# Sorted tokens of a mixture of experts: results scattered back by the row's own number instead of gathered

## The chip, the cores and the metric

The kernel runs on one core of a Trainium2 chip. TensorE is called PE, VectorE DVE, ScalarE ACT, GpSimd POOL and SyncE SP. Times are device microseconds of one launch; the measure is the median of repeated runs. A profile of one execution gives the times of single instructions.

## The reference, cut to what matters

The input is 32 images of 128 channels and 56 x 56 positions, in float32. A binary convolution and an attention-like layer come first. Then each of an image's 3136 positions is a token of 128 values, and a router sends it to two of eight experts:

```python
router_probs = jax.nn.softmax(x @ router_w + router_b, axis=-1)
top_p, top_i = jax.lax.top_k(router_probs, K)          # K = 2 of E = 8
top_p = top_p / jnp.sum(top_p, axis=-1, keepdims=True)
expert_out = jnp.einsum('bnd,edc->bnec', x, expert_w) + expert_b
gathered = jnp.take_along_axis(expert_out, top_i[..., None], axis=2)
return jnp.einsum('bnk,bnkc->bnc', top_p, gathered)
```

The result is added to the token and returned with channels ahead of positions.

## The kernel before, in words

**Two ways through the experts.** An image's tokens are cut into 25 chunks of up to 128 tokens, four chunks to a block. The first chunks of an image go the dense way: all eight experts are computed for every token (`gated` on DVE at L1141, `experts` on PE at L1159), each token's input multiplied by its gates, which SP loads from DRAM spread over all partitions (`spread`, L1132, into the ring `bc` of four buffers). The last 17 or 13 chunks of images 0 to 27 go the sorted way; images 28 to 31 are all dense.

**The sorted way.** Images form four groups of 8, 8, 8 and 4. There are 28 pairs of experts, and each group has a table `rows` in DRAM with a region for each pair. Per image, `pair_of` finds each token's pair and writes `hot`, which has a one at the token's pair (L1256). `places` (L1278 to L1293) finds each token's place in its pair's region by matmuls: `before`, a triangle of ones, counts the tokens ahead of it in its own chunk, and `ones_h` adds the chunks ahead of that one, four chunks at a time through `hot_sum`, which `hot_blocks` makes on POOL for images 0 to 7 (L1268) and on DVE for the others (L1272). `count_on` and `count_rest` keep the running count of the group for the next image. `row_numbers` (L1313 to L1318) turns places into rows. `row_scalars` writes two gates and an offset twice beside the token's 128 values (L1346), and `scatter` (L1365) writes a chunk's rows of 132 values to `rows` with an indirect DMA on POOL.

When a group is full, `list_1` to `list_4` make the list of its tiles, 128 rows of one pair each, and `pad` writes zero rows behind the end of each region. Four tiles make a quad: 40, 40, 32 and 20 quads in the groups, 132 in all. `tile_load` on SP reads a quad, `tile_turn` and `tile_turned` transpose it, `tile_experts` (L1687) multiplies by the two experts, `tile_read` on ACT applies the gates into `v` and `w` (rings of three and two buffers), `tile_sum` and `tile_out` on DVE (L1717, L1722) add them and the token, and `tile_store` on SP (L1730) writes the quad to a table `res` in the order of the tiles.

To bring the results back, `result_rows` on DVE (L1423 to L1439) computes for each token the row of `res` that holds its result; `gather` (L1444) reads each chunk's rows with an indirect DMA on POOL into one of 14 buffers `back`; `back_turn` on PE (L1459), `back_out` on ACT and `back_store` on SP transpose and store a block.

**The order of the work.** All engines run instructions in a written order. A planner makes it ahead of the launch: every step has an engine, a price in microseconds, a due time, the steps it follows and the buffers it takes and frees, and `in_order` lists the steps as if each engine worked through them at these prices, the most urgent of those that could start at about the same time first. `TILE_PACE` and `GATHER_PACE` spread a group's tiles and its gathers over time. On POOL, an indirect DMA also waits for the fourth indirect DMA ahead of it (`in_turn`, `IN_FLIGHT`).

Of the kernel before, what the change touches and what calls it, by code (L numbers as in the profile page):

```python
# [54 lines left out]
C = 128  # L55
# [23 lines left out]
ON_POOL = 8  # L79
# [4 lines left out]
GATE_LANDS, SPREAD_LANDS, STORE_LANDS, TILE_LANDS, GATHER_LANDS = 5.0, 6.5, 5.0, 6.0, 12.0  # L84
TILE_PACE = (0.7, 0.6, 0.4, 0.3)
GATHER_PACE = (1.0, 0.8, 0.5, 0.4)
N_Q = C + 2 * N_EXP
Q_GROUP = 3

# [9 lines left out]
    ps=5, acc=1, ff=2, y=3, qs=3, tt=4, bc=4, gt=2, gated=2,  # L99
    t_in=3, turned=2, v=3, w=2, back=12, sent=4, o=2,  # L100
# [85 lines left out]
def conv_attn_moe_kernel(  # L186
# [45 lines left out]
    n_list = 2  # L232
    assert max(group_rows) // C + N_PAIR <= n_list * C
# [20 lines left out]
    m_one = const.tile([C, 2], F32, name="m_one")  # L254
    nc.vector.memset(m_one, -1.0)


    member = bpool.tile([C, C // GROUP], F32, tag="back", bufs=14, name="member")
# [18 lines left out]
    bk_bc = bpool.tile([C, C], F32, tag="back", bufs=14, name="bk_bc")  # L277
# [147 lines left out]
    no_row = const.tile([C, most], F32, name="no_row")  # L425
    zeros = const.tile([C, ROW], F32, name="zeros")

    count = const.tile([C, N_PAIR], F32, name="count")
    count_h = const.tile([C, 2, N_PAIR], BF16, name="count_h")


    hot_all = const.tile([C, most + 1, N_PAIR], BF16, name="hot")
    hot_sum = const.tile([C, most // PER, N_PAIR], BF16, name="hot_sum")

    def prepare_sorted():
        nc.gpsimd.memset(hot_all, 0.0)
        nc.vector.memset(count_h, 0.0)
# [21 lines left out]
        nc.vector.tensor_scalar(tile_row, tile_no, float(C), None, ALU.mult)  # L459
        nc.vector.memset(no_row, 0.0)  # L460
# [83 lines left out]
    def plan_image(i: int):  # L544
# [578 lines left out]
        def spread(b, k):  # L1123
            n = cols_of(b)[1] - cols_of(b)[0]
            if k == 0:
                gt = bpool.tile([n_g, WIDE], BF16, tag="gt", bufs=2, name=f"gt_{i}_{b}")
                rows = d["gb"][b, :, :, :n].rearrange("j e t -> (j e) t")
                for r in range(0, n_g, n_g // 3):
                    nc.sync.dma_start(gt[r : r + n_g // 3, :n], rows)
                d["gt", b] = gt  # L1130
            bc = bpool.tile([C, 2, WIDE], F32, tag="bc", bufs=4, name=f"bc_{i}_{b}_{k}")
            nc.sync.dma_start(  # L1132
                bc[:, :, :n],
                d["gp"][b, 2 * k : 2 * k + 2, :n].unsqueeze(0).to_broadcast([C, 2, n]),
            )
            d["bc", b, k] = bc
# [93 lines left out]
        group = group_of[i]  # L1230
        first_of_group = i == 0 or group_of[i - 1] != group
        sort = slice(n_dense, n_ck)
        hot = hot_all[:, most - n_sort :, :]
        n_full = n_sort // PER

        def pair_of():
            high, low, pair = (
                spool.tile([C, n_sort], F32, tag=t, bufs=n, name=f"{t}_{i}")
                for t, n in (("high", 1), ("low", 1), ("pair", 13))
# [17 lines left out]
                hot[:, :n_sort, :],  # L1257
# [5 lines left out]
        def hot_blocks():  # L1263
            t = hot[:, : n_full * PER, :].rearrange("p (b k) q -> p b k q", k=PER)
            total = hot_sum[:, :n_full, :]
            with nc.allow_low_precision(reason="numbers up to four"):
                if i < ON_POOL:
                    nc.gpsimd.tensor_tensor(total, t[:, :, 0], t[:, :, 1], ALU.add)  # L1268
                    for k in range(2, PER):
                        nc.gpsimd.tensor_tensor(total, total, t[:, :, k], ALU.add)  # L1270
                else:
                    nc.vector.tensor_reduce(total, t.rearrange("p b k q -> p b q k"), AX.X, ALU.add)  # L1272

        def places():


            p = ps.tile([C, n_sort + 1, N_PAIR], F32, tag="ps", name=f"places_{i}")
            nc.tensor.matmul(p, lhsT=before, rhs=hot, start=True, stop=False)  # L1278
            if not first_of_group:
                for j in range(2):  # L1280
                    nc.tensor.matmul(
                        p,
                        lhsT=ones_h[:1],
                        rhs=count_h[:1, j].unsqueeze(1).to_broadcast([1, n_sort + 1, N_PAIR]),
                        start=False,
                        stop=False,
                    )

            counted = [(hot[:, c, :], c + 1, min(n_sort + 1, c // PER * PER + PER)) for c in range(n_sort)]
            counted += [(hot_sum[:, b, :], (b + 1) * PER, n_sort + 1) for b in range(n_full)]  # L1290
            counted = [(t, lo, hi) for t, lo, hi in counted if lo < hi]
            for t, lo, hi in counted:
                nc.tensor.matmul(  # L1293
                    p[:, lo:hi, :],
                    lhsT=ones_h,
                    rhs=t.unsqueeze(1).to_broadcast([C, hi - lo, N_PAIR]),
                    start=False,
                    stop=lo == counted[-1][1] and hi == counted[-1][2],
# [3 lines left out]
        def count_on():  # L1302
            nc.scalar.copy(count, d["places"][:, n_sort, :])
            nc.scalar.copy(count_h[:, 0], d["places"][:, n_sort, :])

        def count_rest():
            nc.vector.tensor_sub(count_h[:, 1], count, count_h[:, 0])

        def row_numbers():
            shape = [C, n_sort, N_PAIR]  # L1310
            own = spool.tile(shape, F32, tag="own", bufs=1, name=f"own_{i}")
            place = spool.tile([C, n_sort], F32, tag="place", bufs=13, name=f"place_{i}")
            nc.vector.tensor_tensor(own, hot[:, :n_sort, :], d.pop("places")[:, :n_sort, :], ALU.mult)  # L1313
# [7 lines left out]
            d["place"] = place  # L1321

        def row_scalars():
# [3 lines left out]
            def tmp(tag):  # L1327
# [17 lines left out]
            pair_shape = [C, n_sort, 2]  # L1345
            nc.vector.tensor_tensor(  # L1346
                row[:, :, C + 2 : ROW],
                a.unsqueeze(2).to_broadcast(pair_shape),
                m_one.unsqueeze(1).to_broadcast(pair_shape),
                ALU.mult,  # L1350
# [11 lines left out]
        def scatter(c):  # L1362
# [15 lines left out]
            after=[("route_3", i), ("row_numbers", i - 1), ("places", i - 1), ("result_rows", i - 13)],  # L1378
        )
        at(  # L1380
            s + 132.5, ("hot_blocks", i), "POOL" if i < ON_POOL else "DVE",
            2.0 if i < ON_POOL else 0.048 * n_sort, hot_blocks, after=[("pair_of", i)],
        )
        at(
            s + 133, ("places", i), "PE", 0.3 + 0.08 * n_sort, places,
            after=[("hot_blocks", i), ("count_rest", i - 1), ("list_1", group - 1)], take=["ps"],
        )
        at(s + 135, ("count_rest", i), "DVE", 0.10, count_rest, after=[("count_on", i)])
        at(s + 134, ("count_on", i), "ACT", 0.22, count_on, after=[("places", i)])
        at(  # L1390
            s + 137, ("row_numbers", i), "DVE", [0.033 * n_sort, 0.034 * n_sort, 0.09], row_numbers,
            after=[("places", i), ("count_on", i), ("scatter", i - 2, n_ck - 1)],
            free=[("ps", ("places", i))],
# [5 lines left out]
        for k, c in enumerate(range(n_dense, n_ck)):  # L1399
# [6 lines left out]
                s + 140 + 2 * k, ("scatter", i, c), "POOL", 1.5, scatter, c,  # L1406
# [11 lines left out]
        def result_rows():  # L1418

            shape = [C, n_sort, N_PAIR]  # L1420
            own = spool.tile(shape, F32, tag="own2", bufs=1, name=f"own2_{i}")
# [456 lines left out]
```

## Time and profile before

| | |
|---|---|
| three runs | 2249.86, 2259.04, 2283.94 us; median 2259.04 |
| the profiled execution | 2270.18 us, of which the span from first to last instruction is 2268.4 |
| busy in the span | PE 93%, DVE 87%, ACT 68%, POOL 46% |
| granted clock of PE, mean | 0.975 |
| indirect DMAs on POOL | 428 scatters, mean 1225 ns; 428 gathers, mean 1134 ns |
| group 0's tiles, first to last | about 505 to 870 us |
| gathers, first to last | 874 to 2241 us |

In a group's row the columns are line, engine, operation, result and operands, shapes and count; then busy microseconds and the mean of one in ns; then the engine's idle time just before, with what ended it. A row of waits names the engine and line that waited, what it waited for, and the sum, the number and the longest of the waits. The lines are those of the kernel before.

### The profile page before, as it was taken

To read this page: it belongs to the slowest core of one execution; us is meant where nothing else is said; L and a number is where in the kernel's file an instruction comes from. 1 tells how busy PE (TensorE), PEld (TensorE's weight loads), DVE (VectorE), ACT (ScalarE), POOL (GpSimd) and SP (SyncE) were. 2 spreads that over 40 slices of the span, in tenths; PEclk is the share of its full clock that TensorE was granted. 3 is DMA by queue.
4 is the path that set the end of the run, shared out by engine and by line. 5 is a ranking of instruction groups with operands and counts; after the bars stand their busy time and mean duration, and the time that the engine had idled before them with its cause. 6 is when DMAs were issued, how large, how long until landed. Compare 5 with 4: busy or idle time off the path is not lost.

```text
span 2268.4 us, 45320 instructions
## 1 busy us (share of the span) xinstructions
PE 2103.4 (93%) x12074; PEld 1449.1 (64%) x12074; DVE 1970.1 (87%) x6074; ACT 1531.2 (68%) x4917; POOL 1041.1 (46%) x1013
## 2 busy tenths in 40 slices
PE   5899999899999999789999999988999999999888
PEld 2666656557777776457676776655676666676544
DVE  4899999999989999688888889988898798789865
ACT  5667776668888887468777867655877776574311
POOL 3044443333433325466443644676654446233563
PEclk9989999999999999899999999999999999999999
DMA  4155544465665565377667766667767777878788
GB/s 166 30 175 177 167 153 141 138 184 184 203 186 165 176 181 168 110 219 252 194 202 220 226 198 202 215 214 240 225 195 232 217 203 247 249 214 270 222 278 273
DMA packets 324364, 448.58 MB, mean 198 GB/s; under 512 B 61832, under 2 KB 222128, under 8 KB 324112
## 3 DMA queue, kind: packets, MB, share of 16 engines
q1 hardware_dynamic: 294384, 382.80, 54.7%
q0 software_dynamic: 28144, 56.14, 8.2%
q10 hardware_dynamic: 1584, 6.75, 0.8%
q8 instruction: 102, 1.67, 0.3%
q14 instruction: 150, 1.23, 0.2%
HBM read 319.51 MB, written 126.00 MB: 196 GB/s over the span
## 4 chain that ended last, share of the span: by engine, by line
PE 42%; DVE 5%; DMA 3%; issue 2%; ACT 2%; another core or an unknown queue 1%; SPq 0%; POOL 0%; DVEq 0%; ACTq 0%; POOLq 0%
PE ff L1159 14%; PE to L1687 7%; PE cv L642 6%; PE q L863 3%; PE gram L744 3%; PE turn L1669 2%; PE back_ps L1459 2%; PE xt L667 2%; DVE gated L1141 1%; DMA back<-res,res_no 1%; PE l L1114 1%; DMA out_dram<-o 1%; PE ff L1153 1%; DMA bc<-gp 0%
## 5 line engine op out<-in xcount | busy, mean ns | idle before, releaser
L1365 POOL DMA_INDIRECT rows<-tok,row_no x428 | 524.3, 1225 | 570.5 <-ACT tok L1358 235.8
L1159 PE MATMUL ff<-gated,ew_d 128*128 128x512 f32 (+1 forms) x1536 | 711.5, 592 | 23.8 <-DVE gated L1141 19.8
L1444 POOL DMA_INDIRECT back<-res,res_no x428 | 485.4, 1134 | 464.1 <-PE back_ps L1459 264.1
L1141 DVE TENSOR_TENSOR gated<-tt,bc 128x1024 f32<-128x1024 f32 x384 | 450.7, 1180 | 92.2 <-PE ff L1159 29.9
L642 PE MATMUL cv<-xs,w_bin 128*128 128x440 bf16 (+3 forms) x2016 | 429.8, 362 | 18.5 <-ACT xs L599 10.0
L1159 PEld LDWEIGHTS ff<-gated,ew_d 128*128 128x128 f32 x1536 | 274.5, 193 | 258.6 <-issue 202.2
L1705 ACT ACTIVATE v<-to,t_in 128x128 f32<-128x128 f32 x528 | 255.3, 484 | 138.1 <-PE to L1687 74.6
L642 PEld LDWEIGHTS <-w_bin 128*128 128x128 bf16 x2016 | 200.1, 100 | 187.8 <-issue 38.3
L1687 PEld LDWEIGHTS to<-ew_s,turned 128*128 128x128 f32 x2112 | 260.8, 194 | 57.8 <-issue 32.4
L877 ACT ACTIVATE qs<-q,r 128x136 f32<-128x136 f32 (+1 forms) x800 | 247.6, 406 | 70.3 <-PE q L863 35.1
L1687 PE MATMUL to<-ew_s,turned 128*128 x2112 | 273.3, 279 | 18.2 <-ACT turned L1675 8.1
L735 ACT ACTIVATE y<-tok,r 128x128 f32<-128x128 f32 (+1 forms) x800 | 257.0, 428 | 24.3 <-PE gram L744 10.4
L863 PE MATMUL q<-move,x 128*128 128x144 f32 (+1 forms) x1600 | 239.9, 295 | 12.7 <-issue 3.7
L863 PEld LDWEIGHTS q<-move,x 128*128 128x128 f32 (+1 forms) x1600 | 213.6, 193 | 42.4 <-issue 21.1
L744 PEld LDWEIGHTS gram<-y 128*128 128x128 f32 (+1 forms) x1600 | 203.3, 192 | 53.9 <-issue 40.4
L744 PE MATMUL gram<-y 128*128 128x129 f32 (+1 forms) x1600 | 217.8, 281 | 12.9 <-issue 8.1
L682 DVE BATCH_NORM_STATS2 st<-tok 128x6 f32<-128x128 f32 (+1 forms) x800 | 185.4, 279 | 31.9 <-ACT tok L673 26.9
L1712 ACT ACTIVATE w<-to,t_in 128x128 f32<-128x128 f32 x528 | 208.6, 395 | 0.0
L893 DVE BATCH_NORM_STATS2 st<-tok 128x6 f32<-128x128 f32 (+1 forms) x800 | 198.1, 284 | 6.3
L673 ACT COPY tok<-xt 128x512 f32<-128x512 f32 (+1 forms) x224 | 121.2, 561 | 99.9 <-PE xt L667 71.6
L653 DVE SCALAR_TENSOR_TENSOR x<-cv,alpha_col,x 128x448 f32<-128x448 f32 x224 | 151.3, 676 | 40.1 <-PE cv L642 7.2
L890 DVE TENSOR_TENSOR tok<-tok,qs 128x408 f32<-128x408 f32 (+1 forms) x288 | 156.1, 542 | 29.4 <-ACT tok L882 24.1
(229 smaller groups left out, 2896.0 us busy)
## 6 DMA issues: line engine op xcount, KB each, us to landing
bc<-gp SPq DMA_DIRECT2D x368, 512.0 KB
x<-in_x_dram SPq DMA_DIRECT2D x116, 392.0 KB
t_in<-rows SPq DMA_DIRECT2D x528, 66.0 KB
res<-v SPq DMA_DIRECT2D x132, 256.0 KB
out_dram<-o SPq DMA_DIRECT2D x100, 256.0 KB
out_dram<-tt SPq DMA_DIRECT2D x92, 256.0 KB
rows<-zeros SPq DMA_DIRECT2D x116, 66.0 KB
rows<-tok,row_no POOLq DMA_INDIRECT x428
```

The costliest lines, as they stand in the source:

```text
L642: nc.tensor.matmul(cv[:, r0:r1, c0:c1], lhsT=w_bin[:, t, :], rhs=xs[:, b * ROWS + dy + r0 : b * ROWS + dy + r1, dx + c0 : dx + c1], start= ...
L735: nc.scalar.mul(y[:n, j, :C], d["tok"][:n, c, :C], d["r1"][:n, c : c + 1])
L744: nc.tensor.matmul(d["gram"], lhsT=y[:n, j, :C], rhs=y[:n, j, :], start=(c == 0), stop=(c == n_ck - 1),)
L863: nc.tensor.matmul(p[:n, k, :], lhsT=d["x"][:, c * C : c * C + n], rhs=move, start=True, stop=True,)
L877: nc.scalar.mul(qs[:n, k, :], p[:n, k, : C + N_EXP], d["r1"][:n, c : c + 1])
L1141: nc.vector.tensor_tensor(g[:, :, :n], d["tt", b][:, :n].unsqueeze(1).to_broadcast([C, 2, n]), d.pop(("bc", b, k))[:, :, :n], ALU.mult,)
L1159: nc.tensor.matmul(d["ff", b][:, :n], lhsT=ew_d[:, e * C : (e + 1) * C], rhs=g[:, j, :n], start=False, stop=(e == N_EXP - 1),)
L1365: dma = nc.gpsimd.indirect_dma_start(out=groups[group]["rows"], out_offset=bass.IndirectOffsetOnAxis(ap=d["row_no"][:n, c - n_dense : c - ...
L1444: dma = nc.gpsimd.indirect_dma_start(out=d["back", c][:n, :], out_offset=None, in_=groups[group]["res"][: quads_of(group) * WIDE, :], in_o ...
L1687: nc.tensor.matmul(p[:, k, j, :], lhsT=t[:, n * C : (n + 1) * C], rhs=ew_s[:, bass.ds(d["cols", q][j][n], C)], start=True, stop=True,)
L1705: nc.scalar.activation(d["v", q][:, n, :], p[:, k, 0, :], AF.Identity, bias=row[:, C + 2 : C + 3], scale=row[:, C : C + 1],)
L1712: nc.scalar.mul(d["w", q][:, n, :], p[:, k, 1, :], row[:, C + 1 : C + 2])
```

## The change

Four things are changed. The row of a token carries, in its last place, the number of a row in `res` that belongs to the token: a first part of `res` has a row for each place of a tile (for the rows that only fill a tile), and behind it stand the images of the group, chunk by chunk. `tile_out` takes the larger of that number and the number of the row's own place, and `send` writes each tile to `res` with an indirect DMA on POOL, four to a quad, in place of the one `tile_store` on SP. The results of a block then lie in order, so that `fetch`, a plain load on SP, takes the place of `result_rows` and the gathers; `back` has three buffers of a block each in place of 14 of a chunk.

Places are counted by partition first: `run_on` adds up `hot` chunk by chunk within each partition on POOL, `places` then needs two matmuls and, after a group's first image, a third for the running count, and `ranks` on POOL adds the two parts together, one per pair, for `row_numbers` to pick from.

The ring `bc` has five buffers. The planner's prices and paces change with it (`SEND` 1.3 for an indirect DMA that was priced at 1.5, `TILE_PACE` longer for all groups).

```diff
-ON_POOL = 8
+RUN, RANK = 0.20, 0.10
-TILE_PACE = (0.7, 0.6, 0.4, 0.3)
+TILE_PACE = (0.9, 0.8, 0.6, 0.4)
+BACK = 3
+SEND = 1.3
-    ps=5, acc=1, ff=2, y=3, qs=3, tt=4, bc=4, gt=2, gated=2,
-    t_in=3, turned=2, v=3, w=2, back=12, sent=4, o=2,
+    ps=5, acc=1, ff=2, y=3, qs=3, tt=4, bc=5, gt=2, gated=2,
+    t_in=3, turned=2, v=3, w=2, back=BACK, sent=4, o=2,
...
-        def hot_blocks():
...
+        def run_on():
+
+            with nc.allow_low_precision(reason="numbers up to the chunks of an image"):
+                for c in range(n_sort):
+                    nc.gpsimd.tensor_tensor(run[:, c + 1], run[:, c], hot[:, c], ALU.add)
 
         def places():
-            p = ps.tile([C, n_sort + 1, N_PAIR], F32, tag="ps", name=f"places_{i}")
-            nc.tensor.matmul(p, lhsT=before, rhs=hot, start=True, stop=False)
+            p = ps.tile([C, 2, N_PAIR], F32, tag="ps", name=f"places_{i}")
             if not first_of_group:
...
+                nc.tensor.matmul(
+                    p,
+                    lhsT=both,
+                    rhs=count_h.unsqueeze(1).to_broadcast([n_part, 2, N_PAIR]),
+                    start=True,
+                    stop=False,
+                )
+            for j, lhs in enumerate((before, ones_h)):
+                nc.tensor.matmul(
+                    p[:, j], lhsT=lhs, rhs=run[:, n_sort], start=first_of_group, stop=first_of_group or j == 1
+                )
...
+        def ranks():
+            shape = [C, n_sort, N_PAIR]
+            d["own"] = spool.tile(shape, F32, tag="own", bufs=1, name=f"own_{i}")
+            nc.gpsimd.tensor_tensor(
+                d["own"], run[:, :n_sort], counts[:, 0].unsqueeze(1).to_broadcast(shape), ALU.add
+            )
...
-            nc.vector.tensor_tensor(own, hot[:, :n_sort, :], d.pop("places")[:, :n_sort, :], ALU.mult)
+            nc.vector.tensor_tensor(own, hot, own, ALU.mult)
...
+            nc.vector.tensor_scalar(row[:, :, C + 2], a, -1.0, None, ALU.mult)
+            nc.vector.tensor_scalar(
+                row[:, :, C + 3], row_of[:, :n_sort], float(first_row * C), None, ALU.add
+            )
...
-        def result_rows():
...
-        def gather(c):
...
+        def fetch(b):
+            n, cs = rows_of(blocks[b][0]), blocks[b]
+            d["back", b] = bpool.tile([C, PER, C], F32, tag="back", bufs=BACK, name=f"back_{i}_{b}")
+            first = (first_row + cs[0] - n_dense) * C
+            rows = groups[group]["res"][first : first + len(cs) * C, :]
+            nc.sync.dma_start(
+                d["back", b][:n, : len(cs), :], rows.rearrange("(k p) c -> p k c", p=C)[:n]
+            )
...
+            at(
+                due + each * k / n_sort, ("fetch", i, b), "SP", 0.43, fetch, b,
+                after=[("send", group, q, k) for q in range(quads_of(group)) for k in range(PER)]
+                + [("fetch", i, b - 1) if k else ("fetch", i - 1, n_blk - 1)],
+                take=["back"], delay=FETCH_LANDS,
+            )
...
+        nc.vector.tensor_tensor(
+            d["no", q], d["in", q][:, :, C + 3], row_of[:, q * PER : (q + 1) * PER], ALU.max
+        )
...
-    def tile_store(g, q):
+    def send(g, q, k):
...
+        nc.gpsimd.nop()
+        dma = nc.gpsimd.indirect_dma_start(
+            out=d["res"],
+            out_offset=bass.IndirectOffsetOnAxis(ap=d["no", q][:, k : k + 1], axis=0),
+            in_=d["v", q][:, k, :],
+            in_offset=None,
+        )
+        alone(f"res{g}", dma, in_turn(dma))
...
+            for k in range(PER):
+                at(
+                    due + 12 + k, ("send", g, q, k), "POOL", SEND, send, g, q, k,
+                    after=[("tile_out", g, q), ("send", g, q, k - 1) if k else ("send", g, q - 1, PER - 1)]
+                    + ([("fetch", last_of[g - 2], n_blk - 1)] if q == k == 0 and g > 1 else []),
+                    free=[("v", ("tile_read", g, q, 0))] if k == PER - 1 else [], delay=3.0,
+                )
```

## The prediction

> **What bounds the kernel now.** I first read the engine shares of the page, then the busy time in stretches.
>
> ```profile
> PE 2103.4 (93%) x12074; PEld 1449.1 (64%) x12074; DVE 1970.1 (87%) x6074; ACT 1531.2 (68%) x4917; POOL 1041.1 (46%) x1013
> ...
> 140.00:490.00 350.00, 330.72 (x1860) 214.59 (x1858) 343.12 (x1210) 237.63 (x795) 157.02 (x144) 0.99 0.47 153
> 560.00:840.00 280.00, 275.56 (x1812) 205.75 (x1811) 262.58 (x822) 239.97 (x785) 92.98 (x73) 1.00 0.59 175
> 910.00:950.00 40.00, 29.94 (x111) 16.14 (x109) 23.32 (x78) 20.23 (x61) 21.79 (x22) 0.76 0.39 116
> 1400.00:1540.00 140.00, 129.51 (x695) 83.57 (x694) 123.08 (x406) 80.18 (x260) 99.98 (x83) 0.96 0.64 204
> 2100.00:2240.00 140.00, 119.68 (x445) 67.13 (x445) 99.13 (x197) 29.86 (x87) 83.96 (x73) 0.91 0.82 266
> ```
>
> The columns of a stretch are PE, PEld, DVE, ACT and POOL busy, then granted clock, DMA share and GB/s. Before the first tiles (140 to 490 us) DVE is busy 98% and sets the pace; beside the tiles of group 0 (560 to 840) PE is, at 98%; in the last stretch neither is full. So microseconds taken from PE count after about 500 us, and hardly before. POOL is nowhere the bound, yet its queue is in order, and each of its 856 indirect DMAs costs about 0.3 us between instructions on top of its busy time.
>
> Then the waits that end PE's idle time after the start (us in total, times, longest):
>
> ```profile
> PE ff L1159 <- DVE gated L1141: 19.8, 20, 2.6
> PE xt L667 <- DVE x L653: 9.6, 10, 1.7
> ...
> PE to L1687 <- ACT turned L1675: 8.1, 5, 3.4
> ```
>
> Nothing in this list names POOL: before the change nobody on PE's path waits for GpSimd.
>
> **The change part by part.** The profiled execution took 2270.18 us (span 2268.4); the median of the three runs is 2259.04, so I work out a difference and take it from the median.
>
> Places on PE. One image's matmuls stand in the timeline:
>
> ```profile
> 885.06 0.38 PE L1278 MATMUL places<-hot,before 128*128 128x504 bf16 x1
> 885.37 0.60 PE L1281 MATMUL places<-count_h,ones_h 1*128 1x504 bf16 x2
> 885.89 0.55 PE L1293 MATMUL places<-hot,ones_h 128*128 128x84 bf16 x13
> 886.30 0.55 PE L1293 MATMUL places<-hot_sum,ones_h 128*128 128x392 bf16 x4
> 886.68 0.31 PE L1017 MATMUL gt_ps<-ident,gate 128*128 128x128 f32 x1
> ```
>
> From 885.06 to 886.68 are 1.62 us for 17 chunks; the same stretch of a 13-chunk image (1509.26 to 1510.49) is 1.23. 16 x 1.62 + 12 x 1.23 = 40.7 us, less about 2 for the four images that have no running count. In their place come three matmuls of 28 to 56 columns. The nearest rows give 0.03 us each (thirteen in 0.41 us) to 0.26 (two in 0.52): 0.1 to 0.8 us an image; I take 0.3, since each also loads its own weights (96 ns in L1293's rows): 8.4 us. That is -30 us of PE. Eight images have their places before 456 us, where DVE is the bound and hides the saving (8 x 1.3 = 10.6). **-20 us**, between 0 and -30.
>
> DVE. result_rows goes: lines 1423, 1431, 1433, 1437 and 1439 together are 59.9 us. The reduction of hot_blocks for images 8 and later (L1272) goes: 15.9. L1346 (5.3) becomes two instructions of 13 or 17 columns, 28 x 2 x 0.17 = 9.5, and each of 132 tile_outs gets a 128x4 maximum at 0.16 to 0.17 (the 128x8 rows of L1009 took 158 ns): 22.4. Sum -49 us, nearly all after 500 us. There PE sets the pace, so this is worth only what PE waits for DVE: some 54 us in all its rows after the start. Between 0 and -49 (all of it, if DVE were the bound); a quarter, **-12 us**, because DVE's load there falls by about 3% while most waits are single handovers.
>
> Five broadcast buffers. DVE's gated waits 21.7 us in 11 waits for bc<-gp. A fifth buffer lets SP issue one transfer earlier, but the longest waits stand where SP had not reached the transfer (between 1504 and 1532 it issued stores and the 28 zero rows and no bc). 0 to -22; **-8 us**. With this cover gone the wait is the old one.
>
> Gathers become plain loads. 428 indirect gathers leave POOL, 128 loads of up to 256 KB go to SP, from which 132 tile stores of 256 KB leave: SP's issue time is level (out_dram<-o of the same size takes 0.34 to 0.38 us to issue), and so are the bytes, up to the padding. PE waited for gathered rows 8.7 us in all, weight loads included, two waits of 2.26 and 1.71 us in the last 30 us: 0 to -9, **-6 us**.
>
> POOL. In come 528 indirect stores. A scatter took 1225 ns, a gather 1134, each plus 0.30 idle: 528 x 1.525 - 428 x 1.434 = +191 us. run_on is 428 dependent adds of 28 columns. The trace has adds of 112 columns and one-column memsets:
>
> ```profile
> L1270 POOL TENSOR_TENSOR hot_sum<-hot_sum,hot 128x112 bf16<-128x112 bf16 x14 | 7.0, 503 | 1.1
> L1268 POOL TENSOR_TENSOR hot_sum<-hot 128x112 bf16<-128x112 bf16 x7 | 2.9, 416 | 78.2 <-DVE gate L981 44.1 <-DVE hot L1256 21.2 <-PE gv L758 13.0
> ...
> L450 POOL MEMSET pair_no<- 128x1 f32 x28 | 2.5, 88 | 0.0
> ```
>
> So 0.09 to 0.5 us; on the line between 88 and 416 ns, 28 columns take 0.17, with 0.08 between adds as in the old chain 0.25: 4.2 us for 17 chunks, 107 us in all (38 to 215). ranks, 476 columns, is 4.25 x 0.42 = 1.8 us, 46 in all. Hot_blocks leaves 11. POOL ends near 59% busy.
>
> The GPSIMD Engine Reference of the Trainium skill (section "Engine selection") advises against two-input elementwise work here, about twice the Vector engine's time, and its "Specifications" say that the engine shares its SBUF interfaces with DVE. The trace agrees on the sharing: the 545 indirect DMAs that ran beside no gated (L1141) took 1086 ns on average, the 24 that lay beside it for 1.25 us or more took 2195. By the 2.6 cycles at 1.2 GHz of its section "Elementwise" an add of 28 columns would be an estimated 0.06 us plus a fixed part, below my 0.17; by it POOL would have an estimated 40 us less to do, and the sum would change by no more than the 20 us set below.
>
> What the new load costs on the path: now PE's places wait for run_on, DVE's row_numbers for ranks, ACT's tile_read for a v buffer that four stores on POOL must free, and SP's first load of a group for the group's last store. Behind places stand all of PE's matmuls, behind row_numbers all of DVE, behind the load all bc transfers, and each engine takes them in order. The planner's 0.20 and 0.10 per chunk lie under my 0.25 and 0.11: 17 x 0.06 = 1 us an image late. 0 (the order leaves room) to +119 (the first rival below, without the savings); **+20 us**, 28 images at 0.7 us, near the lower end because POOL's mean load leaves four tenths idle.
>
> Sum: -20 - 12 - 8 - 6 + 20 = -26 us, so 2259 - 26 = **2233 us**; the profiled execution would be 2244.
>
> **Rivals.**
>
> POOL becomes the bound beside the tiles of group 0; slower. There the stores have their densest long stage: 160 of them in a planned 432 us (0.9 x 60 x 8 by the code), stretched as now (505 to 870 us for a planned 336, a factor of 1.09) to 471 us, and beside them 7.2 images with 17 scatters each. 282 indirect DMAs at 1.50 us (L1365 between 140 and 490 us: 1202 ns plus 0.30) are 423 us, run_on and ranks 7.2 x 6.2 = 45: 468 of 471. It decides from a mean pitch of (471 - 45) / 282 = 1.51 us on. Scatters waited 0.55 us each for ACT's row_add (235.8 us over 428), in part because there was nothing else to do; half of it makes the pitch 1.77: 282 x 0.27 = +76 us here, and for the 243 of group 1, where the same sum leaves 23 of 419 us free, 243 x 0.27 - 23 = +43. With the savings of 46: +73 us, **2332 us**. For: POOL kept 41 to 43 DMAs in 70 us between 1400 and 1540, but PE lost 10 us there. Against: where DVE is quiet (927 to 942 us) the DMAs took 950 ns, and three v buffers at 11.8 us a quad give 35 us, of which four stores take 6.
>
> SP stands at the first load of a group. It waits there for the last store, and no broadcast passes it. SP issued nothing from 922.9 to 956.0 us before the change, and PE lost 10 us between 910 and 950. Four such stops at 10 us against -26: **2273 us**. For: stores land later on a loaded POOL. Against: loads are needed 15 us or more later, and the order may put them behind other transfers.
>
> The relief is larger. If POOL holds nobody up, PE's 30 us count in full, DVE's at half (25), bc 20, the gathered rows 9: -84, **2175 us**. For: the tiles of a group are spread more evenly over the images, and the stretch 2100 to 2240, where PE idles 20 us, loses its gathers. Against: in the first 490 us DVE keeps its work.
>
> **How the numbers follow.** Chances: the forecast (2200 to 2270) 0.40, POOL the bound 0.24, SP's stops 0.10, the larger relief 0.26. The range of 8 in 10 reaches from a little under the larger relief to the POOL rival: 2155 to 2335. 2% is 45 us, about what a measurement of this kernel can tell from no change: faster means under 2214, slower over 2304. Faster: 0.26 and a quarter of the forecast, 0.36; same: 0.30 + 0.10 = 0.40; slower 0.24.
>
> **What would show it.** PE should be near 2073 us busy with three places matmuls an image; DVE near 1921; POOL 1330 or more. Right for the forecast: hardly a PE or DVE wait that names run_on, ranks or a store. For the POOL rival: POOL full beside group 0's tiles, ACT's v waiting for indirect stores, PE's places for POOL. For SP's stops: gaps in SP's bc issues ahead of a group's first load. What would make me wrong: the written order is made anew from other prices, and its luck alone can move some 1%; or adds of 28 columns that cost as much as those of 112.

## The result, and the profile after

The changed kernel takes 2414.97 us (median of four runs, 2411.73 to 2424.75); beside it the kernel before took 2258.35 (2249.86 to 2283.94). The ratio is 1.071, 95% interval 1.067 to 1.075: slower by 157 us where 26 us of gain were forecast, and outside the range. The profiled execution has a span of 2423.0 us (before: 2268.4): PE is idle 295 us of it in place of 165, and busy 24 us longer.

First the engine shares on the page of after, then, in a second block, its busy time in stretches that were shown of before (PE, PEld, DVE, ACT, POOL busy, granted clock, DMA share, GB/s):

```profile
PE 2127.7 (88%) x11650; PEld 1463.3 (60%) x11650; DVE 1944.6 (80%) x6084; ACT 1533.7 (63%) x4917; POOL 1290.0 (53%) x1545
```

```profile
140.00:490.00 350.00, 316.49 (x1658) 205.80 (x1657) 335.23 (x1162) 226.26 (x756) 176.81 (x240) 0.96 0.42 143
560.00:840.00 280.00, 238.44 (x1381) 171.64 (x1380) 224.25 (x721) 193.05 (x633) 199.17 (x223) 0.93 0.44 140
...
2100.00:2240.00 140.00, 128.88 (x745) 92.21 (x743) 98.80 (x255) 82.75 (x253) 72.84 (x67) 0.98 0.70 213
```

PE has 424 matmuls fewer (12074 before), and yet is busy longer, at a lower clock (0.949 over the span, 0.975 before; a matmul of `experts` takes 605 ns on average, 592 before). The largest loss of these stretches stands beside the tiles of group 0: from 560 to 840 us PE was busy 276 of 280 us and is now busy 238, DVE fell from 263 to 224, ACT from 240 to 193. POOL alone rose, from 93 to 199. (The new pace spreads the tiles, so a stretch doesn't hold quite the same work in both.) From 140 to 490 us PE lost 14 us. The last stretch is better than it was; that isn't where the time went.

The waits that end PE's idle time in the profile of after (us in total, times, longest):

```profile
PE places L1299 <- POOL run L1284: 70.1, 23, 11.4
PE ff L1176 <- DVE gated L1158: 26.8, 22, 4.2
```

Before, no line of this list named POOL. Now the first one does: in 23 of 28 images PE stands at `places` until `run_on` is done. The timelines of POOL and PE of after show one of them (start, duration, what ran, idle time ahead of it):

```profile
749.40 1.11 POOL L1712 DMA_INDIRECT res<-v,no  x1 [0.30 <-issue]
750.54 6.03 POOL L1284 TENSOR_TENSOR run<-run,hot 128x28 bf16<-128x28 bf16 x17
```

```profile
755.80 0.20 PE L1291 MATMUL places<-count_h,both 33*128 33x56 bf16 x1
756.62 0.17 PE L1299 MATMUL places<-run,before 128*128 128x28 bf16 x1 [0.63 <-POOL run L1284]
756.65 0.17 PE L1299 MATMUL places<-run,ones_h 128*128 128x28 bf16 x1
```

`run_on` starts 0.03 us after POOL has issued a store, takes 6.03 us for 17 chunks (planned: 3.4; my figure: 4.2), and PE's two matmuls start within 0.05 us of its end. There are three matmuls an image, where an image of 17 chunks had 20, and each takes some 0.2 us.

### The profile page after: what moved, and what is told of

It is laid out like the page before. It is cut to its first block, busy times and chain, and to the rows that moved or that the text cites. A ratio compares the mean times of both kernels' runs of the same rounds, so it can differ in the third digit from the quotient of the medians.

```text
span 2423.0 us, 45045 instructions
## 1 busy us (share of the span) xinstructions
PE 2127.7 (88%) x11650; PEld 1463.3 (60%) x11650; DVE 1944.6 (80%) x6084; ACT 1533.7 (63%) x4917; POOL 1290.0 (53%) x1545
## 5 line engine op out<-in xcount | busy, mean ns | idle before, releaser
L1712 POOL DMA_INDIRECT res<-v,no x528 | 603.7, 1143 | 372.4 <-issue 153.4
L1176 PE MATMUL ff<-gated,ew_d 128*128 128x512 f32 (+1 forms) x1536 | 729.0, 605 | 43.2 <-DVE gated L1158 26.8
L1370 POOL DMA_INDIRECT rows<-tok,row_no x428 | 512.0, 1196 | 324.6 <-ACT tok L1363 145.1
L659 PE MATMUL cv<-xs,w_bin 128*128 128x440 bf16 (+3 forms) x2016 | 444.5, 369 | 25.4 <-ACT w L1690 9.3
L1176 PEld LDWEIGHTS ff<-gated,ew_d 128*128 128x128 f32 x1536 | 281.8, 197 | 289.8 <-issue 227.6
L1665 PEld LDWEIGHTS to<-ew_s,turned 128*128 128x128 f32 x2112 | 266.3, 197 | 55.4 <-issue 35.9
L1665 PE MATMUL to<-ew_s,turned 128*128 x2112 | 280.2, 282 | 17.9 <-issue 9.0
L894 ACT ACTIVATE qs<-q,r 128x136 f32<-128x136 f32 (+1 forms) x800 | 248.2, 406 | 75.1 <-PE q L880 33.4
L880 PE MATMUL q<-move,x 128*128 128x144 f32 (+1 forms) x1600 | 249.8, 301 | 22.4 <-issue 8.0
L1284 POOL TENSOR_TENSOR run<-run,hot 128x28 bf16<-128x28 bf16 x428 | 126.4, 295 | 257.9 <-DVE gate L998 131.8
L880 PEld LDWEIGHTS q<-move,x 128*128 128x128 f32 (+1 forms) x1600 | 220.1, 197 | 51.2 <-issue 28.2
```

The costliest lines, as they stand in the source:

```text
L659: nc.tensor.matmul(cv[:, r0:r1, c0:c1], lhsT=w_bin[:, t, :], rhs=xs[:, b * ROWS + dy + r0 : b * ROWS + dy + r1, dx + c0 : dx + c1], start= ...
L880: nc.tensor.matmul(p[:n, k, :], lhsT=d["x"][:, c * C : c * C + n], rhs=move, start=True, stop=True,)
L894: nc.scalar.mul(qs[:n, k, :], p[:n, k, : C + N_EXP], d["r1"][:n, c : c + 1])
L1176: nc.tensor.matmul(d["ff", b][:, :n], lhsT=ew_d[:, e * C : (e + 1) * C], rhs=g[:, j, :n], start=False, stop=(e == N_EXP - 1),)
L1370: dma = nc.gpsimd.indirect_dma_start(out=groups[group]["rows"], out_offset=bass.IndirectOffsetOnAxis(ap=d["row_no"][:n, c - n_dense : c - ...
L1665: nc.tensor.matmul(p[:, k, j, :], lhsT=t[:, n * C : (n + 1) * C], rhs=ew_s[:, bass.ds(d["cols", q][j][n], C)], start=True, stop=True,)
```

## The experiments

The kernel before takes 2176 to 2177 us on some chips and 2258 to 2285 on others, so a kernel is given by its ratio to the kernel before on its own chip. The expectations call theories by letters and say what each is. Each kernel with a changed price, pace or part has an order planned anew; I guess that 1% of a difference can come from that, and no run measures it. In the four rows marked "medians" the six times of the kernel before reach from 2247 to 2294 us; beside the two lowest alone the ratios would be some 1% higher (1.075 to 1.10).

| run | what it is | us | before | ratio (95%) |
|---|---|---|---|---|
| pace_alone | before, new `TILE_PACE` | 2209.87 | 2176.20 | 1.016 (1.013 to 1.018) |
| send_alone | stores, loads, new pace; old counting | 2206.93 | 2176.20 | 1.015 (1.012 to 1.017) |
| places_alone | new counting; gathers, old pace | 2232.07 | 2176.20 | 1.028 (1.024 to 1.031) |
| run_priced | after, `RUN` 0.36 | 2288.87 | 2176.20 | 1.052 (1.049 to 1.054) |
| after_again | after | 2436.24 | 2285.06 | 1.065 (1.060 to 1.071) |
| run_pairs | after, `run_on` in 11 or 9 adds | 2431.14 | 2285.06 | 1.066 (1.059 to 1.072) |
| all_priced | after, `RUN` 0.36, `SEND` 1.5 | 2459.55 | 2285.06 | 1.076 (1.070 to 1.081) |
| after_oldpace | after, old `TILE_PACE` | 2495.63 | 2285.06 | 1.092 (1.085 to 1.098) |
| run_dve | after, `run_on` and `ranks` on DVE | 2491.32 | 2283.70 | 1.091 (medians) |
| send_oldpace | as send_alone, old pace | 2466.55 | 2283.70 | 1.080 (medians) |
| send_five_oldpace | the same, five `bc` | 2457.94 | 2283.70 | 1.076 (medians) |
| four_bc | after, four `bc` | 2427.81 | 2283.70 | 1.063 (medians) |
| after_third | after | 2311.33 | 2177.32 | 1.062 (1.059 to 1.066) |
| send_again | as send_alone | 2205.32 | 2177.32 | 1.013 (1.011 to 1.014) |
| places_again | as places_alone | 2229.88 | 2177.32 | 1.024 (1.022 to 1.026) |
| pace_again | as pace_alone | 2211.06 | 2177.32 | 1.015 (1.013 to 1.016) |
| run_slack | after, `RUN` 0.36 and slack | 2265.53 | 2177.21 | 1.041 (1.037 to 1.044) |
| places_slack | places_alone, `RUN` 0.36 and slack | 2203.23 | 2177.21 | 1.011 (1.008 to 1.015) |

### The parts, one by one

`places_alone` is the kernel before with the new counting (`run_on`, `ranks` and what goes with them) and the old gathers; its buffer `place` has 13 copies, because the gathers need the places again. `send_alone` is the other half: own numbers, `send`, `fetch`, the new pace, four `bc` buffers, the old counting. `pace_alone` is one line:

```diff
-TILE_PACE = (0.7, 0.6, 0.4, 0.3)
+TILE_PACE = (0.9, 0.8, 0.6, 0.4)
```

and `run_priced` is the changed kernel with

```diff
-RUN, RANK = 0.20, 0.10
+RUN, RANK = 0.36, 0.10
```

> The kernel before with the new way of counting places alone: run_on and ranks on POOL at the prices 0.20 and 0.10 a chunk, three matmuls; gathers, tile_store, four broadcast buffers and the old paces stay. Theory A, run_on: PE waits for 17 adds that take 5.3 to 6.6 us and are priced 3.4, about 3 us an image, and its clock falls behind the waits: 2340 us (2310 to 2390), some 70 us of PE waiting for run_on. Theory B, the stores: without the stores POOL has room, PE waits little: 2240 us (2215 to 2265). Theory C, the paces of the plan: as B.

> The kernel before with the stores by row number and plain loads alone, at the changed kernel's paces and price of 1.3 for an indirect DMA; the old places and four broadcast buffers. Theory A: without run_on and ranks nothing on PE's path waits for POOL's adds: 2235 us (2200 to 2270). Theory B: 528 stores fill POOL beside the tiles of group 0 and ACT, DVE and PE wait in turn: 2390 us (2350 to 2430). Theory C: also slower, 2350 or more, as the paces are the changed kernel's.

> The kernel before with the changed kernel's TILE_PACE (0.9, 0.8, 0.6, 0.4) alone. Theories A and B: within 2% of before, 2258 us (2225 to 2300). Theory C, that spreading the tiles spoils the order: 2350 us or more.

> The changed kernel with run_on priced at what it takes, 0.36 us a chunk in place of 0.20, so that the plan puts places later; nothing else differs. Theory A: the 70 us that PE waited for run_on fall under 25, and with the clock: 2330 us (2290 to 2365). Theory B: no more than 20 us better, 2405 us (2390 to 2425). Theory C: the order is made anew, within 25 us of 2415.

The stores and loads cost no more than the pace that comes with them (1.015 and 1.016), although they fill POOL. The counting alone costs 2.8%, and its profile shows the wait that after shows. PE's first wait in the profile of places_alone:

```profile
PE places L1286 <- POOL run L1271: 58.8, 21, 6.8
```

With `run_on` priced near what it takes, 45.5 us of the wait were left (14 times) and a ratio of 1.052, between what theories A and B expected.

### Price, chain or pace in the whole

`after_again` is the changed kernel. `run_pairs` keeps its written order and prices, and adds two chunks at a time:

```diff
-                for c in range(n_sort):
-                    nc.gpsimd.tensor_tensor(run[:, c + 1], run[:, c], hot[:, c], ALU.add)
+                m = n_sort // 2
+                two = hot[:, : 2 * m].rearrange("p (b k) q -> p b k q", k=2)
+                ahead = run[:, : 2 * m].rearrange("p (b k) q -> p b k q", k=2)
+                nc.gpsimd.tensor_tensor(pair_sum[:, :m], two[:, :, 0], two[:, :, 1], ALU.add)
+                for b in range(m):
+                    nc.gpsimd.tensor_tensor(run[:, 2 * b + 2], run[:, 2 * b], pair_sum[:, b], ALU.add)
+                nc.gpsimd.tensor_tensor(ahead[:, :, 1], ahead[:, :, 0], two[:, :, 0], ALU.add)
+                nc.gpsimd.tensor_tensor(run[:, n_sort], run[:, n_sort - 1], hot[:, n_sort - 1], ALU.add)
```

`all_priced` has `RUN` 0.36 and `SEND` 1.5, `after_oldpace` the pace of the kernel before.

> The changed kernel itself, unchanged, beside the three that follow, so that traces of one chip can be compared. All theories: 1.07 of the kernel before (1.05 to 1.08).

> The changed kernel in the same written order and at the same prices, but run_on adds by pairs: one wide add of neighbouring chunks, one add a pair, one wide add, one for the odd chunk; 11 instructions in place of 17 (9 in place of 13). By the rows some 4.4 and 3.5 us against 5.7 and 5.2, that is 1.3 to 1.7 us less to wait an image. Theory A, that places waits for a run_on longer than its price: the 70 us of that wait fall to about 30 and the time by 50 us (30 to 90), 1.05 of before. Theory B, that POOL is too full and everything behind it waits whatever run_on takes: at most 15 us better, 1.065 to 1.07.

> The changed kernel with both of POOL's new prices at what they take: run_on 0.36 a chunk in place of 0.20, an indirect DMA 1.5 us in place of 1.3; paces and all else as they are. Theory A: run_on's price alone matters, so as with it alone, 1.05 of before. Theory D, that the plan takes POOL to be faster than it is and every engine that waits for POOL comes too early: another 40 us better than with run_on's price alone, 1.02 to 1.035. Theory B, that POOL has too much to do: no better than 1.05, the longer prices only spread the tiles.

> The changed kernel with the old TILE_PACE (0.7, 0.6, 0.4, 0.3). Theory C, that the new pace costs the 1.6% here that it cost alone: 1.055 of before. Theory B, that POOL is too full beside the tiles: with the tiles closer together the stores press harder, 1.08 or more. Theory A: within 1% of the changed kernel.

PE's wait for `run` in run_pairs, and then PE's first two waits in all_priced:

```profile
PE places L1306 <- POOL run L1291: 33.4, 18, 9.4
```

```profile
PE ff L1176 <- DVE gated L1158: 46.6, 26, 12.0
PE kvc_ps L803 <- DVE kv L794: 25.8, 8, 10.7
```

Half the wait for `run` gone (33.4 us left of 66.4 in after_again), and the time is the same; nearly all of it gone (8.9 us left), and the kernel is 1% slower, with the idle time at other lines. (The prices of all_priced also stretch the stores: the last one of group 0 starts at 1132 us, in after_again at 1076.) So the low price by itself is not the cause: this theory fell. Nor is the pace: with the old one the whole is slower still (1.092).

### The adds off POOL, and the smaller parts

`run_dve` moves the 428 adds and the 28 additions of `ranks` to DVE:

```diff
-                    nc.gpsimd.tensor_tensor(run[:, c + 1], run[:, c], hot[:, c], ALU.add)
+                    nc.vector.tensor_tensor(run[:, c + 1], run[:, c], hot[:, c], ALU.add)
```

with `RUN, RANK = 0.09, 0.034`. `send_oldpace` and `send_five_oldpace` are send_alone with the old pace and four or five `bc` buffers, and `four_bc` is the changed kernel with four.

> The changed kernel with the adds of run_on and the one of ranks on VectorE in place of POOL (428 + 28 instructions, planned at 0.09 us a chunk and 0.034 us a chunk on VectorE); the same counting, the same stores and loads. Theory B (coupling: the counting fails because its two POOL steps stand in one in-order queue with the indirect stores, so PE's places waits for POOL and ACT, DVE and PE lose their lead together): the idle time of PE ahead of places, 70 us, falls under 20, the granted clock comes back, and although VectorE gets some 50 us more of work (428 adds at an estimated 0.08 us and 28 of some 0.6 us) the ratio to the kernel before falls from 1.065-1.07 to 1.00-1.03. Rival D (the stores' and the new pace's own cost and VectorE's load decide, and where the adds are done is indifferent): 1.05 to 1.08. If VectorE becomes the bound by those 50 us: over 1.08, with PE waiting for DVE.

> The stores, loads and own numbers alone, with the kernel before's counting, four broadcast buffers and the pace of the kernel before (0.7, 0.6, 0.4, 0.3). With the new pace this was 1.0147, and the new pace alone was 1.0157 in the same runs. If the stores in place of the gathers cost nothing by themselves: 0.99 to 1.005. If the stores beside group 0's tiles need the slower pace because POOL can't take them faster (28 tiles of four stores each at 1.2 to 1.5 us against a pitch of some 6.5 us): 1.02 to 1.05, with ACT's v waiting for the stores. My first prediction's sum for this part, less gathers and more stores, gave about +0.006.

> As the run before, with five broadcast buffers in place of four. The prediction gave five buffers -8 us (0.3 to 0.4%); theory: 0.003 to 0.006 below the run with four. If the buffers are indifferent: the same within 0.003; if the planner turns the fifth buffer into earlier loads that collide on SP: above it.

> The changed kernel with four broadcast buffers in place of five. The changed kernel unaltered has a ratio of 1.065 to 1.071. If five buffers help as predicted (-8 us): 1.07 to 1.08. If they are indifferent: 1.065 to 1.072. If a fifth buffer is part of the harm (more loads in flight ahead of the counting's): 1.05 to 1.06.

run_dve missed its first expectation by far; the last one, over 1.08 by DVE's load, is nearest. A row of its groups (us busy, mean ns, idle time ahead) and one image in its timeline of DVE say why it can't decide:

```profile
L1284 DVE TENSOR_TENSOR run<-run,hot 128x28 bf16<-128x28 bf16 x428 | 73.9, 173 | 14.8 <-DVE run L1284 1.0
```

```profile
617.48 3.49 DVE L1284 TENSOR_TENSOR run<-run,hot 128x28 bf16<-128x28 bf16 x17
```

The chain takes 3.49 us on DVE, 0.205 a chunk and more than twice its price: 428 x 0.205 = 88 us of DVE's time in place of the 34 that I reckoned with, in blocks of up to 3.5 us for which all else on DVE waits. PE's wait at `places` fell to 24 us (17 times), and the kernel is slower all the same. POOL's load was exchanged for one on an engine nearer to the path, and whether a POOL without the counting would have cured the kernel stays untested. With the old pace the stores are at 1.080, above the 1.05 that was expected at most, and the whole at 1.092, against 1.015 and 1.065 with the new one (the whole on one chip, the stores on two of different kinds); so the slower pace is something the stores need, and its 1.5% is part of their price. Four or five `bc` buffers make no difference that the runs resolve: 2428 us with four in the whole, 2436 with five, in two sets of runs on one chip; 1.080 and 1.076 in the stores alone, where the two sets of times overlap. DVE's wait for these transfers did fall, as the waits of four_bc and then after_again show; it was not on the path:

```profile
DVE gated L1158 <- DMA bc<-gp: 45.5, 31, 4.4
```

```profile
DVE gated L1158 <- DMA bc<-gp: 19.2, 13, 3.6
```

### The whole and the parts on one chip

Up to here the three parts were measured beside 2176 us and the unaltered whole beside 2258 and 2285, and the profiles of the second kind show PE idle times that nothing released (last section). These four put all on one chip.

> The changed kernel unaltered, beside the three parts on the same chip. If the kernel before takes about 2176 us here (the chip without TensorE's unreleased idle time): theory H (TensorE's hold-back around stretches at half clock amplifies lost lead) expects 1.045 to 1.055; theory B (only the parts' coupling in POOL's queue) expects 1.065 to 1.071 on any chip. If the kernel before takes 2250 to 2290 us: 1.06 to 1.075 by both.

> The counting alone (its place values kept for the gathers, four broadcast buffers, old pace), again. Beside a kernel before of about 2176 us: 1.025 to 1.031 as it was. Beside 2250 to 2290 us: theory H expects 1.045 to 1.07, theory B 1.025 to 1.035.

> Stores, loads and own numbers alone with the new pace, again. Beside about 2176 us: 1.012 to 1.018. Beside 2250 to 2290 us: theory H expects 1.03 to 1.07 (with the old pace it was 1.080 there), theory B 1.01 to 1.02.

> The new tile pace alone in the kernel before, again. Beside about 2176 us: 1.013 to 1.019. Beside 2250 to 2290 us: theory H expects 1.00 to 1.03 (it loses little lead: TensorE's idle time was 126 us against 162), theory B 1.013 to 1.019.

The whole costs 6.2% here too, between what two theories expected (1.045 to 1.055 and 1.065 to 1.071), so the kind of chip is not the main cause. And the parts don't add: the counting costs 2229.9 - 2177.3 = 53 us beside the gathers and 2311.3 - 2205.3 = 106 us beside the stores. Beside send_again PE is idle 232 us in place of 131, and its wait for `run` alone is 102. That first wait of PE in after_third, and after it POOL's timeline beside the tiles of group 0 (the first two of the 17 adds lie ahead of it):

```profile
PE places L1299 <- POOL run L1284: 101.9, 26, 9.5
```

```profile
730.04 4.64 POOL L1284 TENSOR_TENSOR run<-run,hot 128x28 bf16<-128x28 bf16 x15
735.17 0.99 POOL L1712 DMA_INDIRECT res<-v,no  x1 [0.48 <-issue]
736.19 1.10 POOL L1315 TENSOR_TENSOR own<-run,counts 128x476 f32<-128x476 bf16 x1
737.45 1.05 POOL L1712 DMA_INDIRECT res<-v,no  x1 [0.17 <-issue]
738.80 1.20 POOL L1712 DMA_INDIRECT res<-v,no  x1 [0.30 <-issue]
740.31 0.97 POOL L1712 DMA_INDIRECT res<-v,no  x1 [0.31 <-issue]
```

POOL mostly goes from one indirect DMA to the next after 0.30 us, the least that it leaves between two of them in this stage; to a step of the counting it goes after 0.03, and from one to the next DMA after 0.17 or 0.48. Its busy share hides that. What it does to the counting shows where DVE writes `hot` and POOL starts `run_on`, first in after_third and then in places_again:

```profile
784.64 0.66 DVE L1273 TENSOR_TENSOR hot<-mark,pair_no 128x476 bf16<-128x476 f32 x1
794.27 5.28 POOL L1284 TENSOR_TENSOR run<-run,hot 128x28 bf16<-128x28 bf16 x17
```

```profile
706.91 0.64 DVE L1260 TENSOR_TENSOR hot<-mark,pair_no 128x476 bf16<-128x476 f32 x1
707.70 6.50 POOL L1271 TENSOR_TENSOR run<-run,hot 128x28 bf16<-128x28 bf16 x17 [17.93 <-DVE gate L982]
```

In after_third stores stand between the two, and `run_on` starts 9.0 us after `hot` is there; in places_again 0.2 us after. In the seven images beside group 0's stores (9 to 15, counted from 0) it is 8.1 to 14.4 us, and PE waits 51 us for `run`; in places_again six of them have 0.2 us and one 4.6, and PE waits 16. In the nine images ahead of the stores `run_on` starts within 0.2 us in both, and PE waits 19 and 13. From the first to the last of group 0's 160 stores, the stretches read (columns as above) in send_again, after_third and, for the tiles of group 0 in the kernel before, from 505 to 870 us:

```profile
528.00:968.00 440.00, 415.22 (x2610) 301.59 (x2609) 407.41 (x1359) 350.55 (x1156) 330.89 (x281) 0.98 0.56 174
```

```profile
541.00:1037.00 496.00, 424.64 (x2511) 312.13 (x2510) 407.01 (x1347) 352.08 (x1166) 367.78 (x407) 0.93 0.50 156
```

```profile
505.00:870.00 365.00, 356.04 (x2313) 266.68 (x2312) 344.17 (x1092) 310.79 (x1021) 129.43 (x102) 1.00 0.61 185
```

With 0.31 us for each indirect DMA (280, 280 and 102 of them) and 0.07 for each add of the counting (126 in after_third), POOL is taken 331 + 87 = 418 of 440 us (95%), 368 + 96 = 464 of 496 (93%), and before 129 + 32 = 161 of 365 (44%). The stores alone already fill it; the counting brings 46 us more, and the stage is longer by 56. Of the 106 us between the two kernels, 13 are there when group 0's stores begin, 69 when they end, and 92 at the end of group 1's (1546 against 1454 us).

### Slack ahead of places

The last two take the wait away by the plan: `run_on` priced at 0.36 a chunk, and its result planned as ready 6 us later, so that PE has other work until then.

```diff
-            after=[("pair_of", i), ("places", i - 1), ("ranks", i - 1)],
+            after=[("pair_of", i), ("places", i - 1), ("ranks", i - 1)], delay=6.0,
```

> The changed kernel with run_on planned at 0.36 us a chunk in place of 0.20 and its result planned as usable 6.0 us after its end in place of at once, so that PE reaches places some 6 us later and has other work till then. Theory S (the wait of an in-order PE for run, planned without slack, is the cost): the wait of places for run falls from 102 us under 12 us, PE's idle time to 130-150 us, and beside a kernel before of 2177 us the ratio falls from 1.062 to 1.01-1.03 (beside 2250-2290 us from 1.065 to 1.02-1.04). Rival T (POOL's queue behind the stores is late by more than that, and what it delays, count_on, ranks, row_numbers and the sorted rows' stores, is late whatever PE does meanwhile): the wait falls, but the ratio stays at 1.045 or more, with the idle time moved to other lines.

> The counting alone (old gathers, old pace, four broadcast buffers) with the same two planned numbers, 0.36 us a chunk and 6.0 us more. Without them it was 1.024 to 1.028 with 50 to 59 us of waits of places for run. Theory S: the wait falls under 8 us, and with PE's 30 us of matmuls and DVE's share less the kernel is at 0.985 to 1.005, as my prediction's term for the counting (-20 us, 0.99) had it; rival T: 1.015 or more.

PE's wait for `run` is 1.3 us in run_slack and 4.0 in places_slack, and that is worth 46 and 27 us (1.062 to 1.041; 1.024 to 1.011). Neither reaches what the theory of the missing slack expected; for the whole the rival's mark of 1.045 is missed by little. Much of what remains in run_slack stands in POOL's queue. The stretch of group 0's stores in run_slack, and then waits in that stretch:

```profile
525.00:1004.00 479.00, 430.43 (x2562) 311.02 (x2561) 411.35 (x1361) 364.43 (x1198) 370.72 (x404) 0.96 0.51 163
```

```profile
ACT v L1683 <- DMA res<-v,no: 34.9, 12, 6.7
...
DVE own L1322 <- POOL own L1315: 30.8, 6, 7.6
...
PE ff L1176 <- DVE gated L1158: 19.8, 8, 7.3
```

The wait for a `v` buffer was 20 us in this stretch of after_third. POOL is taken 371 + 95 = 466 of 479 us, 97%, again 39 us longer than with the stores alone. `ranks` now starts 5.8 to 10.2 us after ACT has copied the counts (0.9 to 3.4 in after_third), with other work of POOL ahead of it; DVE waits for `ranks`, ACT for a `v` buffer that late stores free, and PE for DVE. Beside the gathers the same counting with the same slack costs 26 us, beside the stores 2265.5 - 2205.3 = 60.

So at the new pace it takes both. A full POOL alone costs nothing beyond its pace; a chain that crosses POOL twice costs 53 us, 26 with slack, where POOL is taken 58% (505 to 870 us in places_slack, reckoned as above); beside the stores it costs twice as much, 106 and 60. The gathers had the old pace, though, and the counting beside gathers at the new pace was not run. At the old pace, where the stores alone are at 1.076, the counting adds less: 2495.6 - 2457.9 = 38 us, in two sets of runs on one chip. That is as far as the runs go. Open are the 26 us that the counting costs even with slack and room on POOL, where PE waits 4 us for `run`, and how much of the rest is the planned order's luck. No version beat the kernel before.

## Why the prediction was wrong

**The step that failed** is "+20 us, 28 images at 0.7 us, near the lower end because POOL's mean load leaves four tenths idle". The 0.7 us came from the price gap (1 us an image); PE's wait was 70 us in after and 102 in after_third, 2.5 to 3.6 us an image, and with the stores the counting cost 106 us, near the upper end that I had given, +119. Two things were wrong in it. The mean load was taken over the span, while POOL is taken 93 to 95% just where group 0's tiles and the sorted images meet; I had worked that stage out for the rival and didn't use it for the forecast. And the wait was priced as a lateness of one instruction, while in that stage `run_on` itself started 8.1 to 14.4 us after `hot` in after_third, behind stores and scatters.

**The rival "POOL becomes the bound beside the tiles of group 0"** had the place and the mechanism: POOL full there, ACT's `v` waiting for stores and PE's `places` for POOL all appeared. It reckoned 282 indirect DMAs and 468 us of work; in after_third there were 280 and 464. Its size was off: +73 us, against 157. It took off 46 us of savings that mostly didn't come, and had no term for the pace (34 us). The pitch of a DMA didn't rise (1.184 + 0.31 = 1.49 us, where it assumed up to 1.77). What it didn't reckon with is that the other engines run dry meanwhile: in the two stretches above PE is busy 415 of 440 us with the stores alone and 425 of 496 with the counting, and the granted clock goes from 0.98 to 0.93.

**The pace** had no term. It costs 1.5% alone, 34 us, and with the old one the stores alone are at 1.076 to 1.080.

**Places on PE, -20 us.** The new matmuls take 14.7 us in three rows (L1291 and twice L1299: 4.7, 5.0 and 5.0) where I had 8.4, so 24 us of 38.7 are gone, where I had 30. The gain was eaten by the wait.

**DVE, -49 us of work and -12 of time.** The rows that the change touches lose 86 us and gain 42: -44. DVE's total fell only from 1970.1 to 1944.6; rows that the change doesn't touch took some 6 us more, and the rest I haven't traced. In time nothing came back: PE's waits for `gated` rose from 19.8 to 26.8 us.

**The other rivals.** Transfers end 7 us of PE's idle time in after, and DVE waits 18 us for `bc` (22 before), so SP's stops at a group's first load don't show; and of the larger relief there is nothing.

**Five buffers, -8 us:** nothing. **Gathers to loads, -6 us:** 2211.1 - 2205.3 = -6 at equal pace (-3 in the first set, 2209.9 and 2206.9), with intervals that overlap; right, as far as it can be told.

**POOL's work.** Predicted 1330 us or more, found 1290: stores 1143 ns where I took 1225, `ranks` 1106 ns where I took 1800, and `run_on` 295 ns an add plus the gaps, 0.31 to 0.47 us a chunk and 0.37 on average, where I had 0.25. The 24 DMAs of 2195 ns that I set against those beside no `gated` were picked by an overlap that only a long DMA can have; by the DMA's start, in the kernel before, those beside `gated` took 1512 ns and the others 1095. These rows of after show the counting's part:

```profile
L1284 POOL TENSOR_TENSOR run<-run,hot 128x28 bf16<-128x28 bf16 x428 | 126.4, 295 | 257.9 <-DVE gate L998 131.8
L1315 POOL TENSOR_TENSOR own<-run,counts 128x476 f32<-128x476 bf16 x16 | 17.7, 1106 | 5.8 <-ACT count_h L1306 5.6
```

The warning that I gave, adds of 28 columns that cost as much as those of 112, came half true: 295 ns against 416 to 503. The GPSIMD Engine Reference of the Trainium skill (section "Engine selection") puts two-input elementwise work on GpSimd at about twice VectorE's time; here the same add took 295 ns on POOL and 173 on DVE, `ranks` 1106 and 653, a factor of 1.7. Its 2.6 cycles an element (section "Elementwise") would make an estimated 0.06 us of a 28-column add, a fifth of what it took. A line through the two rows above (28 and 476 columns) leaves an estimated 0.24 us that doesn't grow with the width, though their outputs differ in type.

## What to carry to other kernels

Before a step goes to an engine that has room on average, work out that engine's load in the stage where the step will run, with the gaps that it can't do without (0.30 us from one indirect DMA to the next here). At a pace that suited it, work that hardly anybody on the path waits for filled a queue at little cost (a ratio of 1.013, where the pace alone has 1.015), and a short link of the busiest engine's chain cost 53 us in a queue with room; beside the full queue that link cost 106. Planning more time for the late link moves the wait, and cures only the part that was lateness of the link itself.

## What the hardware showed that was not expected

On the chips where the kernel before takes 2258 us and more, PE stops inside runs of matmuls of one tile, where the profile shows nothing that it waits for. The timeline of PE in after:

```profile
735.92 0.38 PE L684 MATMUL xt<-ident,x 128*128 128x128 f32 x2 [0.83 <-issue]
737.37 0.27 PE L684 MATMUL xt<-ident,x 128*128 128x128 f32 x1 [1.06 <-issue]
...
739.49 1.25 PE L659 MATMUL cv<-xs,w_bin 128*128 128x440 bf16 x3 [1.66 <-issue]
```

PE's idle times of over 0.15 us that no event released make 54 us in after, 33 in the kernel before and 2.6 in after_third. 48 of the 54 us lie within 8 us of a stretch at half clock, before or behind it; what causes them the trace doesn't tell. The ratio hardly shows it (1.071 and 1.065 against 1.062).
